# Two layers of a graph network on one core: VectorE's order in the opening, in place of its order at the last two pairs of heads

## The chip, the cores and the metric

The kernel runs on one core of a Trainium2 chip. The metric is the device time in microseconds (us) of one execution. The engines are named as the profile names them: PE is TensorE's matmul, PEld its weight load, DVE VectorE, ACT ScalarE, POOL GpSimd, SP SyncE, which issues the DMAs.

## The reference

The inputs are x of 64 x 256 x 512 (batch, node, feature), a 256 x 256 adjacency matrix of zeros and ones, and the weights of two layers. Everything is float32.

```python
def reference(x, adj, ...):
    # layer 0
    mi = einsum('bkd,od->bko', x, W[:, :512])
    mj = einsum('bkd,od->bko', x, W[:, 512:])
    a = adj.astype(x.dtype);  deg = a.sum(axis=1)
    x = layernorm(x + deg[None, :, None] * (mi + b) + einsum('ij,bjo->bio', a, mj))
    # layer 1: attention with 8 heads of 64, masked by adj
    q, k, v = heads(x @ Wq.T + bq), heads(x @ Wk.T + bk), heads(x @ Wv.T + bv)
    s = where(adj == 0, -inf, (q @ k.T) / 8)
    return layernorm(x + merge(softmax(s) @ v) @ Wo.T + bo)
```

## The kernel before, in words

The 64 batches are taken in 32 groups g of two. `unshifted_path` does all the work; a second path (`general_path`) is entered only for inputs that the first can't take, and does not run here. Matrix products of 2 x 2 blocks are done in Winograd's way, with seven block products in place of eight, so each product needs sums of blocks on both sides: on the left A11, A12, A22 and the sums S1 to S4, on the right B11, B21, B22 and the differences T1 to T4.

**Layer 0 of one batch.** x is split into a rounded part xhi (ACT, L368) and the remainder xlo (POOL, L370), so that the product with the graph is exact; then POOL adds degb, the bias times the degree, to x in place (L373). The graph product of each of four chunks c goes to a PSUM bank (`pa`), 4 instructions a chunk. `take_input` copies three of its blocks to SBUF (xl, ACT, L486) and forms S1, S3, S2 and S4 on DVE (L489 to L492), each from one operand in PSUM; a bank is free when its last sum has read it. Then seven steps (`l0_steps`) multiply these by blocks of the weights w0, 8 matmul instructions each, into banks named x, w, y and z; steps 1 and 3 share x, 4 and 6 share y, 5 and 7 share z, so step 6 writes the bank that step 4's add has read, and step 7 that of step 5's. The results are added into xh on DVE (L530) and, for step 1, through a copy u1 on POOL (L538). Steps 6 and 7 end with the layer norm of a half each.

**The opening** does layer 0 of batch 0 with nothing to hide behind. SP loads, in this order, the graph, x of batch 0, the blocks B11 of the weights, the bias b_bc, T3, B22, B21 (the slot T3 holds a raw block at first), x of batch 1, and later the raw weights of layer 1. DVE forms the differences T1, T2, T4 (L880) ahead of the sums, and T3 (L882) after them. `first_inputs` multiplies all four chunks by xhi first, then by xlo, two chunks in the banks of the scores and two in the pool of three common banks. `check_graph` (L352 to L356) compares the graph with its float32r copy and makes the mask. `make_factors` forms differences of layer 1's weights on DVE (L411) and stores them to DRAM.

**One turn of the loop** over g: it runs attention over the 8 pairs of heads of group g (`scores`, `values`, divisions by the sums), and in between, as pieces of a list `work`, layer 0 of the two batches of group g + 1. At the last two pairs, `divide_at_once` takes two reciprocals (L815) and two products (L816) that complete aoT, the left factor of the output projection; its blocks' sums S1, S2, S3, S4 are formed on DVE (L470 to L473) into oS. The projection's steps (`o_steps`: first A11, A12, A22, then S2, S1, S3, S4) stand among steps 4 to 7 of layer 0 and the transposes of its result; the first is added by POOL through a copy u1 (L698, L699), the others by DVE (L692). `end_values` adds the reciprocals to rtot on POOL (L821). Then follow q, k and v of group g + 1.

**What sets the order.** A planner in the framework orders the instructions of each engine: those whose operands it believes to be ready, earlier in program order first. `in_order` pins an instruction behind the one traced just before it on its engine; `anywhere` leaves it free. All matmuls are pinned. The planner also gives a tile its buffer from those of its pool that are free. In the kernel before, the last two pairs read as below; `left_steps` makes S1, S2, S3, S4, all pinned, and the adds of steps 4 and 5 of layer 0 are pinned too:

```python
left = left_steps(oS[g], in_order)
run(o[:1] + rest[:1] + o[1:2] + left[:1] + rest[1:2] + left[1:])
end_values(inverses)
run(rest[2:] + o[2:5] + work[SLOTS + 1] + o[5:6] + work[SLOTS + 2] + o[6:])
```

where `o` are the projection's steps and `rest` the steps 4 to 7 of layer 0.

Of the kernel before, what the change touches and what calls it, by code (L numbers as in the profile page):

```python
# [16 lines left out]
P = 128  # L17
# [208 lines left out]
def unshifted_path(ctx, tc, flag, x, adj, wiT, wjT, b0, wqT, bq, wkT, bk, wvT, bv, woT, bo, out):  # L226
# [42 lines left out]
    def score_banks(name):  # L269
        return ps_s.tile([P, 2, 512], F32, tag="sc", name=name)  # L270


    def in_order(ins):

        tc.keep_in_program_order(ins)
# [13 lines left out]
    xh = {}  # L289

    def load_x(b):
        if b < B:
            xh[b] = p6.tile([P, NT, D], F32, tag="xh", name="xh")
            nc.sync.dma_start(out=xh[b], in_=x[b].rearrange("(t p) d -> p t d", p=P))
# [4 lines left out]

    for n, w, j in ((B11, wiT, 0), (T3, wiT, 1), (B22, wjT, 1), (B21, wjT, 0)):  # L300
        nc.sync.dma_start(out=w0[:, n], in_=w.rearrange("(c p) o -> p c o", p=P)[:, :, j * H:(j + 1) * H])
        if n == B11:
            nc.sync.dma_start(out=b_bc, in_=b0.to_broadcast([P, D]))
    load_x(1)


    ident = const.tile([P, P], F32, name="ident")
# [21 lines left out]
    def diagonal(t):  # L329
        return slice(2 * t * P, (2 * t + 1) * P)  # L330

    def edges(t):
        return slice((1 - t) * P, (3 - t) * P)
# [3 lines left out]
    for t in range(NT):  # L337
        pt = bank("pt_a")[:, :N]
        for i in range(NT):
            transpose(pt[:, i * P:(i + 1) * P], a[:, i, t * P:(t + 1) * P], ident)  # L340

        nc.vector.tensor_copy(graph[:, t, edges(t)], pt)
        nc.scalar.copy(aT[:, t, :], pt)

    inexact = const.tile([P, 1], F32, name="inexact")

    def check_graph():


        exact = p1.tile([P, NT, 3 * P], F32, tag="oS", name="exact")  # L350
        for t in range(NT):
            nc.vector.tensor_copy(exact[:, t, edges(t)], aT[:, t, :])  # L352
            nc.vector.tensor_scalar(exact[:, t, diagonal(t)], ident, deg[:, t:t + 1], None, ALU.mult)
        nc.vector.tensor_tensor(exact, exact, graph.bitcast(F32), ALU.not_equal)
        nc.vector.tensor_reduce(inexact, exact.rearrange("p t n -> p (t n)"), AX.X, ALU.max)
        nc.vector.tensor_scalar(maskT, aT, 0.0, MASK, ALU.is_equal, ALU.mult)  # L356

    def degree_bias():
        for t in range(NT):
            in_order(nc.vector.tensor_scalar(degb[:, t, :], b_bc, deg[:, t:t + 1], None, ALU.mult))  # L360

    xhi, xlo, xl, xS, hT, hS, qT, kT, vv, aoT, oS = ({} for _ in range(11))

    def split_x(b):

        if b < B:
            xhi[b] = p1.tile([P, NT, D], F32R, tag="xhi", name="xhi")
            in_order(nc.scalar.copy(xhi[b], xh[b]))  # L368
            xlo[b] = p1.tile([P, NT, D], F32R, tag="xlo", name="xlo")
            in_order(nc.gpsimd.tensor_tensor(xlo[b], xh[b], xhi[b].bitcast(F32), ALU.subtract))  # L370
            if b == 0:
                degree_bias()
            in_order(nc.gpsimd.tensor_tensor(xh[b], xh[b], degb, ALU.add))  # L373


    def load_bias(b, name):
# [89 lines left out]
        return {"A11": a11, "A12": a12, "A21": a21, "A22": a22,  # L466
                "S1": s[:, 0], "S2": s[:, 1], "S3": s[:, 2], "S4": s[:, 3]}

    def left_steps(f, order=anywhere):
        return [lambda: order(nc.vector.tensor_add(f["S1"], f["A21"], f["A22"])),  # L470
                lambda: order(nc.vector.tensor_sub(f["S2"], f["S1"], f["A11"])),
                lambda: order(nc.vector.tensor_sub(f["S3"], f["A11"], f["A21"])),
                lambda: order(nc.vector.tensor_sub(f["S4"], f["A12"], f["S2"]))]  # L473


    def input_tiles(b):
# [28 lines left out]
    def first_inputs(b):  # L505

        input_tiles(b)
        pas = [score_banks("pa")[:, 0, :] if c < 2 else bank("pa") for c in range(NC)]
        for k, part in enumerate((xhi[b], xlo[b])):
            for c in range(NC):  # L510
                for t in range(NT):
                    graph_product(b, c, pas[c], k * NT + t, t, part)
                if k == 1:
                    take_input(b, c, pas[c])

    def l0_steps(b):
        banks = {}

        def product(name, lname, n, first):
            if first:  # L520
                banks[name] = bank("po")[:, :H]
            for c in range(NC):
                matmul(banks[name], xS[b][lname][:, c, :], w0[:, n, c, :], start=(first and c == 0),
                                 stop=(c == NC - 1), skip_group_check=True)

        def place(t, j):
            return xh[b][:, t, j * H:(j + 1) * H]

        def add_to(dst, src, order=anywhere):
            order(nc.vector.tensor_add(dst, src, dst))  # L530

        def step1():
            product("x", "A11", B11, True)
            u1 = p2.tile([P, H], F32, tag="lu", name="u1")
            nc.scalar.copy(u1, banks["x"])

            rest = xh[b].rearrange("p t (j o) -> p (t j) o", j=2)[:, 1:]
            nc.gpsimd.tensor_tensor(rest, rest, u1.unsqueeze(1).to_broadcast([P, 3, H]), ALU.add)  # L538

        def step2():  # L540
            product("w", "A22", T4, True)
            add_to(place(1, 0), banks["w"])

        def step3():
            product("x", "A12", B21, False)
            add_to(place(0, 0), banks["x"])

        def step4():
            product("y", "S2", T2, True)
            add_to(place(0, 1), banks["y"], in_order)  # L550

        def step5():
            product("z", "S1", T1, True)
            add_to(place(1, 1), banks["z"], in_order)

        def step6():
            product("y", "S3", T3, False)
            h = xh[b][:, 1, :].rearrange("p (j o) -> p j o", j=2)
            add_to(h, banks["y"].unsqueeze(1).to_broadcast([P, 2, H]))
            norm(xh[b][:, 1, :])  # L560

        def step7():
            product("z", "S4", B22, False)
            add_to(place(0, 1), banks["z"])
            norm(xh[b][:, 0, :])

        return [step1, step2, step3, step4, step5, step6, step7]

    def h_transpose(b, t, borrow=False):

        g, i = divmod(b, NB)
        if i == 0 and t == 1:
            hT[g] = p1.tile([P, NC, NB * N], F32, tag="hT", name="hT")
            hS[g] = pair_blocks(hT[g], "hS")
        pt = (score_banks("pt_h")[:, 0, :] if borrow else bank("pt_h")).rearrange("p (c n) -> p c n", c=NC)
        for c in range(NC):
            transpose(pt[:, c, :], xh[b][:, t, c * P:(c + 1) * P], ident)
        nc.scalar.copy(hT[g][:, :, i * N + t * P:i * N + (t + 1) * P], pt)
        if t == 0 and i == NB - 1:
            for step in left_steps(hS[g]):  # L580
                step()

    def add_output_bias(b):

# [289 lines left out]
    raw_q, raw_k = load_raw(wqT, "kT"), load_raw(wkT, "oS")  # L874
    load_x(2)
    raw_v, raw_o = load_raw(wvT, "v"), load_raw(woT, "aoT")
    split_x(0)
    w0s = [w0[:, n] for n in range(7)]
    for n, m, k in ((T1, T3, B11), (T2, B22, T1), (T4, B21, T2)):
        in_order(nc.vector.tensor_sub(w0s[n], w0s[m], w0s[k]))  # L880
    first_inputs(0)
    in_order(nc.vector.tensor_sub(w0s[T3], w0s[B22], w0s[T3]))  # L882
    p, q = l0_steps(0), l0_steps(1)
    run([p[0], p[2], p[1]])
    split_x(1)
    run(p[3:5])
    bias_steps()
    make_factors(wqT, "wq", raw_q)
    run(p[5:])
# [30 lines left out]
    for g in range(NG - 1):  # L920
        load_x(NB * (g + 2))
        load_x(NB * (g + 2) + 1)
        work = layer0(g + 1)
        run(work[0])
        for w in range(2, NB * NC, 2):
            values(g, w - 2)
            values(g, w - 1)
            multiply()
            divide_two(g, w - 1)
            later = [scores(g, w), scores(g, w + 1)]  # L930
            part = work[w // 2]
            n = 0 if w == NB * NC - 2 else 1
            run(later[:n] + part[:1] + later[n:] + part[1:])
        w = NB * NC - 2
        values(g, w)
        values(g, w + 1)
        multiply()
        inverses = divide_at_once(g, w + 1)
        o = o_steps(g)
        rest = work[SLOTS]  # L940
        left = left_steps(oS[g], in_order)
        run(o[:1] + rest[:1] + o[1:2] + left[:1] + rest[1:2] + left[1:])
        end_values(inverses)
        run(rest[2:] + o[2:5] + work[SLOTS + 1] + o[5:6] + work[SLOTS + 2] + o[6:])
        end = finish_steps(g)
        q = qk_steps(g + 1, qT, "qT", bq_sb, bqd)
        k = with_output_bias(g + 1, qk_steps(g + 1, kT, "kT", bk_sb, bkd))
        v = v_steps(g + 1)
        run(q[:5] + end[:1] + q[5:6] + end[1:2] + q[6:7] + end[2:3] + k[:1] + end[3:4] + k[1:] + end[4:] + v[:1])
        split_x(NB * (g + 2))  # L950
        run(v[1:5])
        run([scores(g + 1, 0), scores(g + 1, 1)])
        run(v[5:])
# [93 lines left out]
```

## Time and profile before

| | us |
|---|---|
| median of 6 runs | 3220.16 |
| lowest and highest | 3217.01, 3222.06 |
| the profiled execution's own time | 3221.36 |
| its span, first to last instruction | 3219.2 |

The mean granted clock of PE in the profiled execution is 0.998. The span has an opening of about 31 us up to layer 0 of the second batch, a stretch to about 90 us in which the first q, k and v are made and the weights' factors stored, 31 turns of 99.28 us each, and the last group, which has no next layer 0. A line of the timeline gives start and duration in us, engine, line, operation, the tiles written and read, shapes, count, and in brackets how long the engine stood idle just before and what ended that. A line of the waits gives who waited for whom, the total in us, how often, and the longest.

### The profile page before, as it was taken

To read this page: it belongs to the slowest core of one execution; us is meant where nothing else is said; L and a number is where in the kernel's file an instruction comes from. 1 tells how busy PE (TensorE), PEld (TensorE's weight loads), DVE (VectorE), ACT (ScalarE), POOL (GpSimd) and SP (SyncE) were. 2 spreads that over 40 slices of the span, in tenths; PEclk is the share of its full clock that TensorE was granted. 3 is DMA by queue.
4 is the path that set the end of the run, shared out by engine and by line. 5 is a ranking of instruction groups with operands and counts; after the bars stand their busy time and mean duration, and the time that the engine had idled before them with its cause. 6 is when DMAs were issued, how large, how long until landed. Compare 5 with 4: busy or idle time off the path is not lost. (4 is left out here: it accounts for less than half of the span.)

```text
span 3219.2 us, 48188 instructions
## 1 busy us (share of the span) xinstructions
PE 3180.9 (99%) x17398; PEld 2620.0 (81%) x17398; DVE 1847.2 (57%) x3847; ACT 1108.6 (34%) x2146; POOL 1504.8 (47%) x1191
## 2 busy tenths in 40 slices
PE   7999999999999999999999999999999999999998
PEld 6888888888888888888888888888888888888885
DVE  6655555555565555655555655556555565555655
ACT  2333333333333433333333333333333333333333
POOL 3454444544445444455444454344544445444453
PEclk9999999999999999999999999999999999999999
DMA  7234332333323433223442234432334323333222
GB/s 245 65 107 125 121 95 75 103 118 123 111 65 95 121 122 119 74 87 112 123 123 86 77 107 122 121 106 67 100 119 124 113 69 91 118 121 119 80 71 93
DMA packets 257167, 340.89 MB, mean 106 GB/s; under 512 B 29856, under 2 KB 154272, under 8 KB 256928
## 3 DMA queue, kind: packets, MB, share of 16 engines
q1 hardware_dynamic: 256928, 337.76, 34.2%
q8 instruction: 143, 2.34, 0.3%
q14 instruction: 96, 0.79, 0.1%
HBM read 274.73 MB, written 37.75 MB: 97 GB/s over the span
## 5 line engine op out<-in xcount | busy, mean ns | idle before, releaser
L454 POOL TENSOR_TENSOR rstd<-ve,mhalf 128x1 f32<-128x1 f32 x256 | 139.5, 549 | 802.5 <-DVE below L452 802.5
L281 PE MATMUL po<-w,xS 128*128 128x256 f32 x2048 | 466.2, 381 | 0.5 <-DVE xh L530 0.5
L281 PE MATMUL st<-hS,factor 128*128 128x256 f32 x2048 | 454.4, 380 | 2.7 <-DVE u L637 2.7
L764 POOL TENSOR_TENSOR pk<-pe 128x512 f32<-128x512 f32 x256 | 321.9, 1273 | 276.9 <-ACT pe L761 276.9
L281 PEld LDWEIGHTS po<-w,xS 128*128 128x128 f32 x2048 | 386.7, 190 | 62.6 <-DVE rden L834 10.3
L281 PEld LDWEIGHTS st<-hS,factor 128*128 128x128 f32 x2048 | 390.2, 191 | 56.5 <-DVE u L637 3.1
L281 PE MATMUL po<-w,xl 128*128 128x256 f32 x1536 | 360.4, 384 | 17.3 <-DVE xS L492 16.4
L761 ACT ACTIVATE pe<-pe 128x1024 f32<-128x1024 f32 x256 | 270.2, 1057 | 248.2 <-DVE pe L757 248.2
L281 PEld LDWEIGHTS po<-w,xl 128*128 128x128 f32 x1536 | 284.2, 190 | 73.9 <-PE po L281 23.1
L281 PE MATMUL st<-hT,factor 128*128 128x256 f32 x1536 | 342.2, 379 | 1.0 <-DVE qT L668 1.0
L757 DVE TENSOR_TENSOR pe<-ps,maskT 128x1024 f32<-128x1024 f32 x256 | 297.1, 1201 | 67.6 <-PE ps L281 67.6
L637 DVE TENSOR_TENSOR u<-st,u 128x512 f32<-128x512 f32 x96 | 66.4, 692 | 468.6 <-PE st L281 461.1
L530 DVE TENSOR_TENSOR xh<-po,xh 128x256 f32<-128x256 f32 (+1 forms) x384 | 172.5, 463 | 279.6 <-POOL xh L538 197.0
L281 PEld LDWEIGHTS st<-hT,factor 128*128 128x128 f32 x1536 | 291.7, 190 | 40.9 <-DVE qT L668 1.4
L281 PE MATMUL ps<-qT,kT 64*128 64x256 f32 x2048 | 256.5, 389 | 0.0
L281 PE MATMUL pav<-pe,v_sb 128*64 128x256 f32 x2048 | 250.1, 386 | 1.9 <-ACT pe L761 1.8
L281 PEld LDWEIGHTS ps<-qT,kT 64*128 64x128 f32 x2048 | 187.0, 186 | 68.2 <-issue 51.3
L281 PE MATMUL st<-factor,hS 128*128 128x256 f32 x1024 | 234.8, 382 | 0.0
L281 PE MATMUL st<-factor,oS 128*128 128x256 f32 x992 | 229.4, 379 | 0.0
L692 DVE TENSOR_TENSOR xh<-st,xh 128x512 f32<-128x512 f32 x186 | 144.9, 779 | 134.9 <-PE st L281 133.8
L834 DVE RECIPROCAL rden<-den 128x256 f32<-128x256 f32 x96 | 168.7, 1757 | 92.0 <-PE den L281 86.3
L281 PEld LDWEIGHTS st<-factor,hS 128*128 128x128 f32 x1024 | 191.9, 190 | 35.4 <-issue 10.6
(112 smaller groups left out, 4920.7 us busy)
## 6 DMA issues: line engine op xcount, KB each, us to landing
xh<-in_x_dram SPq DMA_DIRECT2D x64, 512.0 KB, 4.1
factor<-wq SPq DMA_DIRECT2D x128, 256.0 KB, 2.6
factor<-wk SPq DMA_DIRECT2D x128, 256.0 KB, 2.6
factor<-wv SPq DMA_DIRECT2D x128, 256.0 KB, 4.4
factor<-wo SPq DMA_DIRECT2D x124, 256.0 KB, 2.7
out_dram<-xh SPq DMA_DIRECT2D x62, 512.0 KB, 4.1
factor<-in_wqT_dram SPq DMA_DIRECT2D x96, 256.0 KB, 2.7
factor<-in_wkT_dram SPq DMA_DIRECT2D x96, 256.0 KB, 2.7
```

The lines of the kernel that those rows point to most:

```text
L281: in_order(nc.tensor.matmul(*args, **kw))
L454: nc.gpsimd.tensor_tensor(rstd, ve, mhalf, ALU.pow)
L530: order(nc.vector.tensor_add(dst, src, dst))
L637: nc.vector.tensor_add(new("u2"), bank["y"], k["u1"])
L692: nc.vector.tensor_add(dst, src, dst)
L757: nc.vector.tensor_add(pe.rearrange("p j t q -> p j (t q)"), ps.rearrange("p j t q -> p j (t q)"), maskT.rearrange("p t q -> p (t q)").uns ...
L761: in_order(nc.scalar.activation(flat, flat, AF.Exp, scale=QSCALE, accum_out=etot[:, NB * g + i, pr:pr + 1]))
L764: nc.gpsimd.tensor_tensor(pk, pe[:, :, 0, :], pe[:, :, 1, :], ALU.add)
L834: nc.vector.reciprocal(rden, den)
```

## The change

In the opening: x of batch 0 is rounded right after the loads are issued, and the copies of aT on ACT are pinned behind that. The remainder of batch 0 is made on DVE (`remainder(0, nc.vector)`) instead of POOL. The bias b_bc is loaded behind all four blocks of the weights. `first_inputs` takes its chunks in reverse, puts one of them in the bank of the values and only one in the common pool, and returns a function that forms the sums by name: S3 and S2 of all chunks, then S1, then S4. DVE's order is pinned: remainder, T1, T2, T4, the sums S3 and S2, the degree bias, S1, the difference T3, S4. POOL's add of the degree bias follows the sums S3 and S2. The graph check is pinned where it is written, the second batch's split is written in two pieces.

At the last two pairs of heads: `left_steps` becomes `combine_left`, written after step 5 of layer 0, with only S3 pinned; the adds of steps 4 and 5 are no longer pinned.

```diff
@@ loads, in program order
     for n, w, j in ((B11, wiT, 0), (T3, wiT, 1), (B22, wjT, 1), (B21, wjT, 0)):
         nc.sync.dma_start(out=w0[:, n], ...)
-        if n == B11:
-            nc.sync.dma_start(out=b_bc, in_=b0.to_broadcast([P, D]))
+    nc.sync.dma_start(out=b_bc, in_=b0.to_broadcast([P, D]))
     load_x(1)
+    def round_x(b):
+        xhi[b] = p1.tile([P, NT, D], F32R, tag="xhi", name="xhi")
+        in_order(nc.scalar.copy(xhi[b], xh[b]))
+    round_x(0)
...
-        nc.scalar.copy(aT[:, t, :], pt)
+        in_order(nc.scalar.copy(aT[:, t, :], pt))
...
@@ check_graph: each of its instructions is now in_order(...)
...
+    def remainder(b, engine):
+        xlo[b] = p1.tile([P, NT, D], F32R, tag="xlo", name="xlo")
+        in_order(engine.tensor_tensor(xlo[b], xh[b], xhi[b].bitcast(F32), ALU.subtract))
+    def add_bias(b):
+        in_order(nc.gpsimd.tensor_tensor(xh[b], xh[b], degb, ALU.add))
...
-    def left_steps(f, order=anywhere):
-        return [lambda: order(nc.vector.tensor_add(f["S1"], f["A21"], f["A22"])),
-                lambda: order(nc.vector.tensor_sub(f["S2"], f["S1"], f["A11"])),
-                lambda: order(nc.vector.tensor_sub(f["S3"], f["A11"], f["A21"])),
-                lambda: order(nc.vector.tensor_sub(f["S4"], f["A12"], f["S2"]))]
+    def combine_left(f, order=anywhere):
+        nc.vector.tensor_add(f["S1"], f["A21"], f["A22"])
+        nc.vector.tensor_sub(f["S2"], f["S1"], f["A11"])
+        order(nc.vector.tensor_sub(f["S3"], f["A11"], f["A21"]))
+        nc.vector.tensor_sub(f["S4"], f["A12"], f["S2"])
...
@@ first_inputs
-        pas = [score_banks("pa")[:, 0, :] if c < 2 else bank("pa") for c in range(NC)]
+        pas = [score_banks("pa")[:, 0, :], score_banks("pa")[:, 0, :],
+               ps_v.tile([P, 2, N], F32, tag="av", name="pa").rearrange("p r q -> p (r q)"), bank("pa")]
+        f = xS[b]
         for k, part in enumerate((xhi[b], xlo[b])):
-            for c in range(NC):
+            for c in reversed(range(NC)):
                 for t in range(NT):
                     graph_product(b, c, pas[c], k * NT + t, t, part)
                 if k == 1:
-                    take_input(b, c, pas[c])
+                    in_order(nc.scalar.copy(xl[b][:, c].rearrange("p m n -> p (m n)"), pas[c][:, :3 * P]))
+        def add(name, c, x, y, sign):
+            in_order(nc.vector.tensor_tensor(f[name][:, c], x, y, ALU.add if sign > 0 else ALU.subtract))
+        def sums(name):
+            for c in reversed(range(NC)):
+                _, a12, a22, a21 = (pas[c][:, m * P:(m + 1) * P] for m in range(4))
+                if name == "S2":
+                    add("S3", c, f["A11"][:, c], a21, -1)
+                    add("S2", c, a22, f["S3"][:, c], -1)
+                elif name == "S1":
+                    add("S1", c, a21, f["A22"][:, c], 1)
+                else:
+                    add("S4", c, a12, f["S2"][:, c], -1)
+        return sums
...
@@ l0_steps, steps 4 and 5
-            add_to(place(0, 1), banks["y"], in_order)
+            add_to(place(0, 1), banks["y"])
-            add_to(place(1, 1), banks["z"], in_order)
+            add_to(place(1, 1), banks["z"])
...
@@ the opening
-    split_x(0)
+    remainder(0, nc.vector)
+    sums = first_inputs(0)
     w0s = [w0[:, n] for n in range(7)]
     for n, m, k in ((T1, T3, B11), (T2, B22, T1), (T4, B21, T2)):
         in_order(nc.vector.tensor_sub(w0s[n], w0s[m], w0s[k]))
-    first_inputs(0)
+    sums("S2")
+    degree_bias()
+    add_bias(0)
+    sums("S1")
     in_order(nc.vector.tensor_sub(w0s[T3], w0s[B22], w0s[T3]))
+    sums("S4")
     p, q = l0_steps(0), l0_steps(1)
     run([p[0], p[2], p[1]])
-    split_x(1)
+    round_x(1)
+    remainder(1, nc.gpsimd)
     run(p[3:5])
+    add_bias(1)
     bias_steps()
...
@@ the last two pairs of heads
-        left = left_steps(oS[g], in_order)
-        run(o[:1] + rest[:1] + o[1:2] + left[:1] + rest[1:2] + left[1:])
+        run(o[:1] + rest[:1] + o[1:2] + rest[1:2])
+        combine_left(oS[g], in_order)
         end_values(inverses)
```

The sums of hS, left unpinned in both kernels, are written through the same function.

More of the change, by code (lines that the diff above doesn't have):

```diff
@@ L301, in unshifted_path @@
         nc.sync.dma_start(out=w0[:, n], in_=w.rearrange("(c p) o -> p c o", p=P)[:, :, j * H:(j + 1) * H])
-        if n == B11:
-            nc.sync.dma_start(out=b_bc, in_=b0.to_broadcast([P, D]))
+    nc.sync.dma_start(out=b_bc, in_=b0.to_broadcast([P, D]))
     load_x(1)
+    xhi, xlo, xl, xS, hT, hS, qT, kT, vv, aoT, oS = ({} for _ in range(11))
+    def round_x(b):
+        xhi[b] = p1.tile([P, NT, D], F32R, tag="xhi", name="xhi")
+        in_order(nc.scalar.copy(xhi[b], xh[b]))
+    round_x(0)
     ident = const.tile([P, P], F32, name="ident")
@@ L351, in check_graph @@
         for t in range(NT):
[L352 to L356, printed above, removed]
+            in_order(nc.vector.tensor_copy(exact[:, t, edges(t)], aT[:, t, :]))
+            in_order(nc.vector.tensor_scalar(exact[:, t, diagonal(t)], ident, deg[:, t:t + 1], None, ALU.mult))
+        in_order(nc.vector.tensor_tensor(exact, exact, graph.bitcast(F32), ALU.not_equal))
+        in_order(nc.vector.tensor_reduce(inexact, exact.rearrange("p t n -> p (t n)"), AX.X, ALU.max))
+        in_order(nc.vector.tensor_scalar(maskT, aT, 0.0, MASK, ALU.is_equal, ALU.mult))
     def degree_bias():
@@ L360, in degree_bias @@
             in_order(nc.vector.tensor_scalar(degb[:, t, :], b_bc, deg[:, t:t + 1], None, ALU.mult))
-    xhi, xlo, xl, xS, hT, hS, qT, kT, vv, aoT, oS = ({} for _ in range(11))
+    def remainder(b, engine):
[3 more added lines that the diff above has]
+        in_order(nc.gpsimd.tensor_tensor(xh[b], xh[b], degb, ALU.add))
     def split_x(b):
         if b < B:
[L367 to L373, printed above, removed]
+            round_x(b)
+            remainder(b, nc.gpsimd)
+            add_bias(b)
     def load_bias(b, name):
@@ L527, in place, with add_to @@
             return xh[b][:, t, j * H:(j + 1) * H]
-        def add_to(dst, src, order=anywhere):
-            order(nc.vector.tensor_add(dst, src, dst))
+        def add_to(dst, src):
+            nc.vector.tensor_add(dst, src, dst)
         def step1():
@@ L579, in h_transpose @@
         if t == 0 and i == NB - 1:
-            for step in left_steps(hS[g]):
-                step()
+            combine_left(hS[g])
     def add_output_bias(b):
```

## The prediction

> **What bounds the kernel now.** I read four views in this order: the page's busy times, the list of who waited for whom with TensorE (PE) as the waiter, the timeline of the first 36 us, and the timeline of one turn of the loop around the last two pairs of heads. The first fence is the page's line, the second is from the list of waits (total us, times, longest us).
>
> ```profile
> PE 3180.9 (99%) x17398; PEld 2620.0 (81%) x17398; DVE 1847.2 (57%) x3847; ACT 1108.6 (34%) x2146; POOL 1504.8 (47%) x1191
> ```
>
> ```profile
> PE po L281 <- DVE xS L492: 16.4, 32, 4.9
> ...
> PE st L281 <- DVE u L637: 2.7, 1, 2.7
> ```
>
> PE is busy for 3180.9 of 3219.2 us, so a microsecond of VectorE (DVE) or GpSimd (POOL) work counts only where PE stands still for it. PE waits 32 times for the last sums of layer 0 (L492): 4.9 us once, in the opening, and (16.4 - 4.9) / 31 = 0.37 us in each of the 31 turns of the loop. The reciprocals at L815 recur every 99.28 us with hardly any scatter: a turn is paced by PE. So a turn can gain at most that 0.37 us, which lies at the second half of layer 0's inputs, a place that the change does not touch. The loop has something to lose and almost nothing to win; the opening can win.
>
> The opening, from the timeline (start, us, engine, line):
>
> ```profile
> 7.37 2.37 POOL L370 TENSOR_TENSOR xlo<-xh,xhi 128x1024 fp32r<-128x1024 f32 x1 [5.66 <-ACT xhi L368]
> ...
> 10.56 2.38 POOL L373 TENSOR_TENSOR xh<-xh,degb 128x1024 f32<-128x1024 f32 x1 [0.82 <-DVE degb L360]
> 10.60 3.42 DVE L880 TENSOR_TENSOR w<-w 128x1024 f32<-128x1024 f32 x1 [0.18 <-DMA w<-in_wiT_dram]
> ...
> 14.29 3.96 DVE L880 TENSOR_TENSOR w<-w 128x1024 f32<-128x1024 f32 x2
> ...
> 21.17 3.56 PE L281 MATMUL po<-w,xl 128*128 128x256 f32 x8 [4.86 <-DVE xS L492]
> ...
> 24.53 7.20 PE L281 MATMUL po<-w,xS 128*128 128x256 f32 x32
> ```
>
> The first weight difference takes 3.42 us where the same instruction alone takes about 1.1: it starts while POOL's add (10.56 to 12.94) runs and ends 1.08 us after it. The next two end at 18.25, so the 16 sums start at 18.18, the PSUM bank that PE wants comes free late, and PE stands 4.86 us. After that its 8 matmuls start 0.427 us apart instead of 0.216 (the granted clock is 0.83 in the mean of 20 to 30 us).
>
> The end of a turn, from the same view:
>
> ```profile
> 1036.62 1.89 PE L281 MATMUL st<-factor,aoT 128*128 128x256 f32 x8
> 1036.99 2.35 POOL L699 TENSOR_TENSOR xh<-xh,u 128x1024 f32<-128x1024 f32 x1
> 1037.14 0.42 DVE L816 TENSOR_TENSOR aoT<-pav,rden 128x256 f32<-128x256 f32 x1
> 1037.48 0.41 DVE L530 TENSOR_TENSOR xh<-po,xh 128x256 f32<-128x256 f32 x1
> ...
> 1038.35 5.34 PE L281 MATMUL po<-w,xS 128*128 128x256 f32 x24
> ...
> 1038.62 0.69 DVE L692 TENSOR_TENSOR xh<-st,xh 128x512 f32<-128x512 f32 x1 [0.73 <-PE st L281]
> 1039.23 0.68 DVE L470 TENSOR_TENSOR oS<-aoT 128x512 f32<-128x512 f32 x1
> 1039.30 1.19 POOL L821 TENSOR_TENSOR rtot<-rtot,rden 128x256 f32<-128x256 f32 x1
> 1040.28 0.42 DVE L530 TENSOR_TENSOR xh<-po,xh 128x256 f32<-128x256 f32 x1 [0.37 <-PE po L281]
> 1040.62 0.68 DVE L471 TENSOR_TENSOR oS<-oS,aoT 128x512 f32<-128x512 f32 x1
> ```
>
> The 24 matmuls from 1038.35 are steps 5, 6 and 7 of layer 0, 8 each, 0.216 apart: step 7 begins at 1041.80. It goes on in the bank of step 5, so step 5's add (L530 at 1040.28, ending 1040.70) must have read it: 1.1 us to spare. Likewise step 4's add (ends 1037.89) before step 6 at 1040.08. DVE waits 0.73 us before L692 with S1 (L470) pinned behind it, and S1 starts just as POOL's L699 ends at 1039.34.
>
> **The loop's part.** The change takes the pins off the adds of steps 4 and 5 and off S1, S2 and S4; S3 stays pinned behind S2, and the sums are traced behind step 5. It adds and removes no instruction here. What is not pinned goes where the planner believes its operands to be ready, earlier in the text first. How it places such sums is seen at the same sums of hS (L470, L472, L471, then L692, then L473, from 1052.22): as early as the operands allow, with other work slipped in between. Here S1 needs only the second product of L816. In the planner's order it comes ahead of o's second add (L692) if the planner has L816 done before PE has finished that product: in the trace 1037.56 (1037.9 if step 4's add slips in front) against 1038.5. The planner's reciprocals cannot be much slower than real, nor below some 1 us: it put the second sum of rtot (L821) behind L698 and L699, so its second reciprocal ended after u1 was there, about 2.5 us after the first began. So I take the order step 4, S1, L692, S2, S3, step 5, S4.
>
> Now that order with the chip's durations. S1 reads two SBUF tensors and is issued near 1037.9, while L699 holds until 1039.34. By the row of L880 it ends 0.60 after that, at 1039.94, as it does today; what is new is that L692 now stands behind it: 1040.55, S2 1041.15, S3 1041.75, step 5's add 1042.15. Step 7 would begin at 1041.80, so PE waits 0.4; if POOL's rtot sum (0.73 us alone) slips in between S1 and S2, as it can during L692, which reads PSUM (the sums L489 to L492 do too, and keep their 0.28 beside POOL's L796 at 1018.62), some 0.2 more. Behind that the norm is 0.3 to 0.5 later and has 1.7 us of slack (second ACT apply of the first row ends 1046.74, PE needs it at 1048.49): nothing more. I take 0.5 a turn, 31 x 0.5 = 15.5 us. Bounds: 0 if the planner has L692 first (today's timing, a gain being excluded since PE does not wait there); 1.1 if S4 also goes ahead of step 5 (0.6 more); 1.4 if short planned reciprocals put S1 and S2 ahead of step 4's add too, which then misses step 6 at 1040.08.
>
> [...]
>
> **The opening's part**, piece by piece. x rounded first: 0; ACT's rounding starts at 6.24 today, when x lands (6.19), and the copies of aT that go behind it feed nothing early. Remainder on DVE: 7.34 to about 8.5 (1.1 to 1.2, the L880 rows) instead of POOL's 9.74, but PE takes it at 10.07 after 8 half-speed products: 0 again, yet POOL is now idle when the weight differences run. Bias behind the weights: the landings are 1.5 us apart (7.55, 9.05, 10.51, 12.03, 13.51), so T3, B22 and B21 land at about 9.05, 10.5 and 12.0, the bias at 13.5. The three differences then end near 10.2, 11.7 and 13.2 (today 18.25). Chunks reversed: the copy of chunk 0 is the last of ACT's four (ends 12.70 today), so the first product starts 0.7 late, at 12.7; A12 15.0 to 16.7; A22 with T4 16.7 to 18.5, without today's wait. On DVE: 8 sums of 0.2 to 14.8, degree bias 1.3 to 16, four sums to 16.8; then T3's difference stands behind POOL's add of that bias (2.4, to 18.4) and ends at 19.5; the last four sums 20.3. The bank for step 4 frees with the first of these, 19.9 (its bank is chunk 3's), PE having stood 1.4 us. Four steps of 1.73 end at 26.8; today layer 0's next inputs start at 31.35. That is 4.5 us earlier.
>
> Given back: make_factors' four L411 (0.6 each) now meet POOL's second remainder and add (2.4 each); the add of step 6 stands behind them, near 28.6 where the third bank is wanted near 29.0: 0.5. The graph check, now wholly pinned with its mask (0.41) moved to it, stands before step 4 of the second batch, where PE already waits 0.53 at 45.42: 0.4. Left: about 3.5 us. Bounds: +1 (4.5 lost if POOL and DVE block each other further) to -6.
>
> The idle 1.4 us could also halve the clock. The rows: 0.97 us of idleness (67.18) costs one slow step, 2.72 us (78.80) brings half speed for some 8 matmuls, 1.7 us. I take no slowing, as nearer to the first. [...]
>
> **Sum.** The profiled execution took 3221.36 us (span 3219.2 and 2.2 around it), 1.2 above the median 3220.16. On it: 3221.4 + 15.5 - 3.5 = 3233.4; less 1.2, 3232 for the median.
>
> **Rivals.** What a measurement can tell from no change is about 0.2%, 6.4 us.
> (1) Chance 0.38, the forecast: S1 ahead of L692 only, 0.4 to 0.65 a turn, 3229 to 3237.
> (2) Chance 0.22: S4, or S1 and S2, also ahead of the adds, 1.1 to 1.4 a turn, +31 to +40: 3251 to 3260. For it: planned reciprocals may be short. Against: step 5's product is ready (1040.24) just when S3 would end without POOL.
> (3) Chance 0.25: taking the pins off does not change DVE's order where it matters, L692 still comes first, and only the opening counts: 3216.7, within 0.2%. For it: S1 and L692 become ready within 0.6 us of each other.
> (4) Chance 0.15, the faster side: as (3), and the opening's lead also swallows waits after it, of PE at 36.26 (0.41), 67.18 (0.97) and 78.80 (2.72 with 1.7 of half clock). It decides from 2.9 us on top of the 3.5; all of them would make 3211. Against it: each follows work that moves along.
>
> Chances: faster 0.15, within 0.2% 0.25, slower 0.60. The range leaves out most of (4) and the top of (2): 3213 to 3256; the likeliest case alone is 3229 to 3237.
>
> **What would show it.** Right: L470 starting near 1037.9 of a turn and lasting 2 us, L692 behind it, a new wait "PE po <- DVE xh L530" 31 times, 0.4 to 0.65 each; turns of 99.7 to 99.9 us. In the opening L880 at 1.1 to 1.2 us each, the 4.86 gone, layer 0's second inputs near 27. Wrong: turns still at 99.28, or L470 short while POOL runs.

## The result, and the profile after

| | before | after |
|---|---|---|
| median (us) | 3220.12 (36 runs) | 3227.18 (16 runs) |
| lowest, highest | 3216.66, 3223.74 | 3226.81, 3229.16 |
| span of the profiled execution | 3219.2 | 3226.0 |
| reciprocal that opens the last two pairs, first turn, at | 139.29 | 134.62 |
| median turn of the loop | 99.281 | 99.668 |

The ratio is 1.0024, 95% interval 1.0018 to 1.0031: slower by 7 us, a little over what a measurement can tell from no change. The prediction was 3232 us, slower with chance 0.60. The last two rows of the table part the result for the two profiled executions: the loop begins 4.67 us earlier, loses 11.64 us over the 31 turns that follow (0.387 in the median turn), and the last group's first reciprocal comes 6.97 us late.

The page's line of the engines, after:

```profile
PE 3186.6 (99%) x17398; PEld 2615.4 (81%) x17398; DVE 1891.1 (59%) x3848; ACT 1112.0 (34%) x2146; POOL 1502.1 (47%) x1190
```

DVE is busy 44 us longer for one instruction more. That is the sign of a DVE instruction that stands still while it counts as busy: 44 / 31 = 1.4 us a turn, as long as S1 grew (0.68 to 2.09 below).

The list of waits, with PE as the waiter and then, from the same list, with PE's weight load (total us, times, longest us):

```profile
PE po L281 <- DVE xS L501: 11.2, 31, 0.7
...
PE po L281 <- ACT xl L495: 1.9, 1, 1.9
...
PE po L281 <- DVE xS L528: 1.2, 1, 1.2
...
PE po L281 <- DVE xh L557: 0.9, 1, 0.9
```

```profile
PEld po L281 <- DVE xh L557: 17.5, 32, 1.3
```

The 4.9 us of the opening are gone (1.2 at L528 is what is left of them), the 0.36 a turn at layer 0's inputs stayed (L501, before L492), and a wait for DVE's adds into xh (L557, before L530) is new, 31 times in the loop. It stands under the weight load, since the load for step 7's first matmul is what is held; PE's own list has L557 once, with 0.9 us, and would not have shown it.

The opening's timeline, DVE and PE:

```profile
7.39 1.23 DVE L373 TENSOR_TENSOR xlo<-xh,xhi 128x1024 fp32r<-128x1024 f32 x1 [1.47 <-ACT xhi L310]
...
9.40 1.23 DVE L907 TENSOR_TENSOR w<-w 128x1024 f32<-128x1024 f32 x1 [0.78 <-DMA w<-in_wiT_dram]
...
12.40 1.23 DVE L907 TENSOR_TENSOR w<-w 128x1024 f32<-128x1024 f32 x1 [0.28 <-DMA w<-in_wjT_dram]
...
17.21 2.88 DVE L912 TENSOR_TENSOR w<-w 128x1024 f32<-128x1024 f32 x1
...
20.43 7.14 PE L281 MATMUL po<-w,xS 128*128 128x256 f32 x32 [1.17 <-DVE xS L528]
...
33.97 2.37 PE L281 MATMUL po<-w,xl 128*128 128x256 f32 x9 [1.93 <-ACT xl L495]
```

The weight differences take 1.23 us each where the first took 3.42, and the third ends at 13.6, not 18.25. T3's (L912) stands behind POOL's add (16.65 to 19.00) as foreseen. PE has step 4 at 20.43 instead of 24.53, at full clock (granted 1.00 from 20 to 28 us, where before had 0.67 from 20 to 24 and 0.90 from 24 to 28). The last row is a place where time is given back.

One turn, DVE, POOL and the weight load (the first reciprocal of the turn is at 1031.62):

```profile
1035.43 2.36 POOL L725 TENSOR_TENSOR xh<-xh,u 128x1024 f32<-128x1024 f32 x1
...
1036.25 2.09 DVE L479 TENSOR_TENSOR oS<-aoT 128x512 f32<-128x512 f32 x1
...
1037.74 1.18 POOL L847 TENSOR_TENSOR rtot<-rtot,rden 128x256 f32<-128x256 f32 x1
1038.26 0.68 DVE L718 TENSOR_TENSOR xh<-st,xh 128x512 f32<-128x512 f32 x1
1038.86 0.68 DVE L480 TENSOR_TENSOR oS<-oS,aoT 128x512 f32<-128x512 f32 x1
1039.46 0.68 DVE L481 TENSOR_TENSOR oS<-aoT 128x512 f32<-128x512 f32 x1
1040.06 0.41 DVE L557 TENSOR_TENSOR xh<-po,xh 128x256 f32<-128x256 f32 x1
1040.39 0.68 DVE L482 TENSOR_TENSOR oS<-aoT,oS 128x512 f32<-128x512 f32 x1
1040.53 1.59 PEld L281 LDWEIGHTS po<-w,xS 128*128 128x128 f32 x8 [0.53 <-DVE xh L557]
```

S1 (L479) is issued early, stands until POOL's add (L725) is through at 1037.79 and ends 0.55 later. Behind it come o's second add (L718), S2, S3 and only then the add of step 5 (L557), which ends 8.85 us after the turn's first reciprocal; before, it ended 7.5 after it, and step 7 started 8.62 after it. The weight load stands 0.53 us for it; 0.39 of that is lost to the turn.

### The profile page after: what moved, and what is told of

The parts are those of the page before. It is cut to its first block, busy times and chain, and to the rows that moved or that the text cites. A ratio compares the mean times of both kernels' runs of the same rounds, so it can differ in the third digit from the quotient of the medians.

```text
span 3226.0 us, 48220 instructions
## 1 busy us (share of the span) xinstructions
PE 3186.6 (99%) x17398; PEld 2615.4 (81%) x17398; DVE 1891.1 (59%) x3848; ACT 1112.0 (34%) x2146; POOL 1502.1 (47%) x1190
## 5 line engine op out<-in xcount | busy, mean ns | idle before, releaser
L281 PE MATMUL po<-w,xS 128*128 128x256 f32 x2048 | 474.4, 382 | 5.8 <-DVE xS L528 1.2
L281 PEld LDWEIGHTS po<-w,xS 128*128 128x128 f32 x2048 | 383.8, 190 | 78.8 <-DVE xh L557 17.5
L663 DVE TENSOR_TENSOR u<-st,u 128x512 f32<-128x512 f32 x96 | 66.4, 692 | 468.0 <-PE st L281 461.5
L557 DVE TENSOR_TENSOR xh<-po,xh 128x256 f32<-128x256 f32 (+1 forms) x384 | 170.3, 457 | 267.3 <-POOL xh L565 197.9
L468 ACT ACTIVATE shift<-below,rstd 128x1 f32<-128x1 f32 x256 | 75.4, 295 | 416.9 <-POOL rstd L463 410.1
```

The lines of the kernel that those rows point to most:

```text
L281: in_order(nc.tensor.matmul(*args, **kw))
L468: order(nc.scalar.activation(shift, below, AF.Identity, scale=rstd))
L663: nc.vector.tensor_add(new("u2"), bank["y"], k["u1"])
```

## The experiments

"After" is the changed kernel. The experiments ran in three groups, each beside runs of the kernel before: e1 to e4 (before: median 3219.3 us), e5, e7, e8 and m1 (3220.14), e6, e9, e10 and e11 (3219.39). A ratio is that to the kernel before of the same group.

**The two parts, each alone.** After, with the loop's old code (e1, "the opening alone" below):

```diff
-        run(o[:1] + rest[:1] + o[1:2] + rest[1:2])
-        combine_left(oS[g], in_order)
+        left = left_steps(oS[g], in_order)
+        run(o[:1] + rest[:1] + o[1:2] + left[:1] + rest[1:2] + left[1:])
```

and the adds of steps 4 and 5 pinned again:

> The changed kernel with the old order at the last two pairs of heads: sums S1 to S4 pinned, S1 ahead of step 5's add, the adds of steps 4 and 5 pinned. Theory (the loop costs 0.385 us a turn, the opening gives 4.7 us, and the two add up): turns of 99.28 us, first reciprocal of the last two pairs at 134.6 us, 3220.1 - 4.7 = 3215.4 us, ratio to the kernel before 0.9985. Rival (the opening's lead is an effect of the new loop order, or is lost later): first reciprocal near 139 us or a ratio of 1.000.

And the kernel before, with only the loop's new code (e2):

> The kernel before with only the order at the last two pairs of heads changed (sums of oS unpinned but S3, adds of steps 4 and 5 unpinned); its opening is the old one. Theory: turns of 99.66 to 99.67 us, S1 lasting 2.1 us, 3220.1 + 31 x 0.385 = 3232.0 us, ratio 1.0037. Rival (part of the loss comes from the new opening, by a shifted phase of buffers): turns nearer to 99.28 us, ratio under 1.002.

Measured: the opening alone 3215.79 (ratio 0.9989, 0.9980 to 0.9998), turn 99.279, first reciprocal 133.64 where 134.6 was expected; the loop alone 3229.96 (1.0030, 1.0018 to 1.0042), turn 99.664, S1 at 2.08 us in the median. That is -3.5 and +10.7, together +7.2 where both gave +7.1: the parts add up, and the whole loss is the loop's.

**Is it the place of the sums?** After, with S1 to S4 pinned behind step 5's add, the adds left free (e4):

```diff
-        run(o[:1] + rest[:1] + o[1:2] + rest[1:2])
-        combine_left(oS[g], in_order)
+        run(o[:1] + rest[:1] + o[1:2] + rest[1:2] + left_steps(oS[g], in_order))
```

> The changed kernel with all four sums of oS pinned in a row behind step 5's add, the adds of steps 4 and 5 unpinned. DVE's order: step 4's add, L719, step 5's add, S1, S2, S3, S4. Theory (what costs is only that step 5's add stands behind S1 and S1 behind POOL): PE does not wait at step 7; S4 ends near 10.0 us after the first reciprocal, the add of step 6 is 0.7 us later than in the kernel before, inside its slack of 1.7 us; turns 99.28 us, 3215.4 us, ratio 0.9985. Rival (the sums are needed early, as in the old order with S1 ahead of step 5): a new wait of PE at the projection's S2 product or at the transposes, turns over 99.5 us.

Measured: 3215.81 (0.9990, 0.9981 to 0.9999), turn 99.275. Its timeline:

```profile
1033.45 0.69 DVE L719 TENSOR_TENSOR xh<-st,xh 128x512 f32<-128x512 f32 x1 [1.26 <-PE st L281]
...
1034.75 0.42 DVE L557 TENSOR_TENSOR xh<-po,xh 128x256 f32<-128x256 f32 x1 [0.61 <-PE po L281]
1035.09 0.68 DVE L479 TENSOR_TENSOR oS<-aoT 128x512 f32<-128x512 f32 x1
```

DVE again waits for PE here instead of PE for DVE, and S1 takes 0.68. It is the old turn with the change's opening.

**Or the missing pins on the adds?** After, only these pins put back (e10):

```diff
-            add_to(place(1, 1), banks["z"])
+            add_to(place(1, 1), banks["z"], in_order)
```

and the same for step 4:

> The changed kernel with the pins put back on the adds of steps 4 and 5 alone; the sums of oS stay written behind step 5 and unpinned. Theory (what counts is that the first sum stands ahead of the projection's second add and of step 5's add): DVE's order around the sums is that of the changed kernel, so the turn stays at 99.67 and the time near 3227. Rival (the missing pins on the adds are the cause): turn 99.28, time 3216.

Measured: 3227.59 (1.0023, 1.0014 to 1.0032), turn 99.664. Step 4's add now stands behind the second product, not ahead of it; from S1 on the order is that of after, S1 takes 2.08 us, and step 5's add ends at 8.85 again (first reciprocal of this turn at 1032.81):

```profile
1037.44 2.08 DVE L479 TENSOR_TENSOR oS<-aoT 128x512 f32<-128x512 f32 x1
...
1041.25 0.41 DVE L557 TENSOR_TENSOR xh<-po,xh 128x256 f32<-128x256 f32 x1
```

The pins on the adds are not the cause; the sums' place is.

**Is it POOL that holds S1?** After, o's add on POOL in two halves (e3):

```diff
-            nc.gpsimd.tensor_tensor(o, o, k["u1"].unsqueeze(2).to_broadcast([P, NT, 2, H]), ALU.add)
+            for t in range(NT):
+                nc.gpsimd.tensor_tensor(o[:, t], o[:, t], k["u1"][:, t].unsqueeze(1).to_broadcast([P, 2, H]), ALU.add)
```

> The changed kernel with POOL's add of 1024 elements of the output projection (L725, 2.35 us) split into two of 512 (about 1.27 us each), nothing left out. DVE's order stays S1, L718, S2, S3, step 5's add, S4. Theory (S1 waits for the end of the POOL instruction in flight, and step 5's add is late by that): S1 lasts about 1.0 us in place of 2.08, S2 may wait for the second half and last about 1.2; step 5's add ends at 8.5 us after the first reciprocal in place of 8.85; PE's wait there is gone or under 0.1 us; turns 99.28 to 99.4 us, 3215 to 3219 us. Rival (the order alone costs it, three sums ahead of step 5's add): S1 unchanged or not, the add ends where it did, turns 99.67 us, 3227 us.

Measured: 3225.22 (1.0018, 1.0009 to 1.0027), turn 99.592, a miss. S1 did get through before POOL's second half was done (1035.88 against 1037.02); but the time came back further down:

```profile
1034.07 2.95 POOL L726 TENSOR_TENSOR xh<-xh,u 128x512 f32<-128x512 f32 x2
...
1034.88 1.00 DVE L479 TENSOR_TENSOR oS<-aoT 128x512 f32<-128x512 f32 x1
1035.80 0.68 DVE L718 TENSOR_TENSOR xh<-st,xh 128x512 f32<-128x512 f32 x1
1036.40 1.16 DVE L480 TENSOR_TENSOR oS<-oS,aoT 128x512 f32<-128x512 f32 x1
1036.97 1.18 POOL L848 TENSOR_TENSOR rtot<-rtot,rden 128x256 f32<-128x256 f32 x1
1037.48 1.21 DVE L481 TENSOR_TENSOR oS<-aoT 128x512 f32<-128x512 f32 x1
1038.62 0.41 DVE L557 TENSOR_TENSOR xh<-po,xh 128x256 f32<-128x256 f32 x1
```

S1 meets the first half, S2 the second, S3 the sum into rtot (L848). In each case the DVE sum ends 0.55 us after POOL's instruction (1037.02 and 1037.56 for S2; 1038.15 and 1038.69 for S3), as S1 does in after. That named the next edit (e5): as e3, with the rtot sums moved behind step 7's norm and pinned there.

> The changed kernel with the 1024-element add split in two (as in e3) and the two sums of rtot on POOL moved behind step 7's norm; nothing left out, DVE's order as in the changed kernel. In e3 S1 fell from 2.08 to 1.00 us, but S2 (1.16) and S3 (1.21) then waited for the second half and for rtot's sum. Theory (each DVE sum of two SBUF tensors waits for the POOL instruction in flight, whichever it is): S1 1.0, S2 1.15, S3 0.68, step 5's add ends near 8.25 us after the first reciprocal, before PE needs it at 8.62; turns 99.28 us, 3216 us. Rival (the order S2, S3 ahead of step 5's add costs by itself): turns 99.6 us, 3225 us.

Measured: 3216.27 (0.9988, 0.9979 to 0.9997), turn 99.284. Its timeline:

```profile
1031.87 0.98 DVE L479 TENSOR_TENSOR oS<-aoT 128x512 f32<-128x512 f32 x1
...
1033.38 1.15 DVE L480 TENSOR_TENSOR oS<-oS,aoT 128x512 f32<-128x512 f32 x1
1034.45 0.68 DVE L481 TENSOR_TENSOR oS<-aoT 128x512 f32<-128x512 f32 x1
1035.05 0.41 DVE L557 TENSOR_TENSOR xh<-po,xh 128x256 f32<-128x256 f32 x1
```

Step 5's add ends 8.23 after the first reciprocal (at 1027.23 in this turn), in time for 8.62. DVE's order is exactly that of after; only POOL's work stands elsewhere. So the order alone does not cost the 0.39 us: it is the order together with the time that sums of two SBUF tensors take beside POOL. S1 to S3 took 2.09, 0.68 and 0.68 us in after, 1.00, 1.16 and 1.21 in e3, and take 0.98, 1.15 and 0.68 here.

**What in the opening brings the 3.5 us?** All three are the opening alone with one edit. The bias loaded behind B11 again (e6):

```diff
-    nc.sync.dma_start(out=b_bc, in_=b0.to_broadcast([P, D]))
+        if n == B11:
+            nc.sync.dma_start(out=b_bc, in_=b0.to_broadcast([P, D]))
```

> The new opening with the old loop, and only the bias' load put back behind the block B11, so that the three other blocks land 1.5 us later. Theory (the load's place is worth what PE's wait before step 4 grows by): the three differences still take 1.23 us each, but the third ends 1.5 us later (near 14.2 where the opening alone has 12.8), all sums follow, PE waits about 2.7 us instead of 1.2 before step 4, first reciprocal of the loop 1.5 later than with the opening alone (133.64), so near 135.1, or near 136.5 if that wait halves the clock; time 1.5 to 3 us over the opening alone. Rival: the differences are not what PE waits for, first reciprocal within 0.5 of 133.64.

The same, with the degree bias and POOL's add of it put ahead of the weight differences (e7):

```diff
     remainder(0, nc.vector)
+    degree_bias()
+    add_bias(0)
...
     sums("S2")
-    degree_bias()
-    add_bias(0)
```

> e1 (the new opening, the old loop) with the bias loaded early again, and with the degree bias and POOL's add of it put back between the remainder and the weight differences, so that POOL runs beside them. Theory (most of the opening's gain is that the differences no longer meet POOL): the first difference starts near 10.5 and ends near 13 or later in place of 10.6, the other two follow to about 16.5, the last sums move by some 3 us, PE waits over 3 us before step 2 or step 4, layer 0's second inputs start near 30 in place of 27; first reciprocal near 136.5, 3218 to 3219 us. Rival (the gain is the order of the sums and the one bank of the common pool): first reciprocal under 135, 3216 us.

And the remainder on POOL (`remainder(0, nc.gpsimd)`, e9):

> The new opening with the old loop, and only the remainder of batch 0 put back on POOL (2.4 us instead of 1.23). Theory: it ends near 8.9, PE wants it at 9.2; the first difference on DVE, due at 8.5, waits for it by some 0.5 us and the second, due at 10.0, not at all, so first reciprocal 133.6 within 0.5 and the time that of the opening alone. Rival (the engine of the remainder is a part of the gain, since POOL's other work follows it): POOL's add or DVE's differences are late by 1 us or more and the first reciprocal is at 134.6 or later.

Measured: bias early 3217.38 (0.9992, 0.9983 to 1.0001), first reciprocal 135.51 against 133.64; with the collision 3217.45 (0.9992, 0.9983 to 1.0001), 135.27; remainder on POOL 3215.86 (0.9988, 0.9979 to 0.9997), 133.43. With the bias early, PE's timeline reads:

```profile
21.18 8.77 PE L281 MATMUL po<-w,xS 128*128 128x256 f32 x32 [3.10 <-DVE xS L529]
```

The wait before step 4 is 3.10 (the opening alone: 0.97) and the 32 matmuls take 8.77 instead of 7.14, at half clock for a while (granted 0.66 in the mean of 20 to 25 us); of these 3.8 us only 1.6 to 1.9 reach the loop, since later waits take up the rest. For e6 the two forecast starts of the loop (135.1 and 136.5) lie on either side of what came. So the load's place is worth 1.6 us of the 3.5 by the medians, the remainder's engine nothing. The intervals against the kernel before are wider than such differences (0.0009 is 2.9 us); what supports the 1.6 is the longer wait in the trace and the later first reciprocal. The collision that I saw in the trace of before (3.42 us) shows no cost once the bias is early: there the three differences took 5.34 us together, but the degree bias then no longer stood between the sums, and PE waited 3.00. Neither of the two starts of the loop forecast for e7 (136.5, or under 135) came. The remaining 1.9 us (order of the sums, chunks reversed, graph check, rounding) was not parted.

**Where the opening gives back.** The opening alone, with batch 0's norm on ACT put behind the four copies of the second batch's inputs (`run(late)` after `l0_inputs(1, 1)`, e8):

> e1 with ACT's two norm applications of batch 0 pinned behind the four copies of the second batch's inputs; in the changed kernel the fourth copy stands behind the first norm and PE waits 1.9 us for it at 33.97. Theory (that wait is the order on ACT alone): the copy ends near 31.5, PE's wait there is gone, first reciprocal 1.0 to 1.9 us earlier than in e1 (133.6), 3214 to 3215 us. Rival (the transposes of batch 0, which need the norm, become late in turn): PE waits at the transposes instead and the first reciprocal stays within 0.5 us.

Measured: 3215.97 (0.9986, 0.9977 to 0.9995), no gain; first reciprocal 133.68. The rival's number came, but not at the place that it named. The wait for ACT's copy went, and a wait of the same length came, for the sums that read the same bank:

```profile
33.57 1.97 PE L281 MATMUL po<-w,xl 128*128 128x256 f32 x8 [1.86 <-DVE xS L501]
```

**The wait that both kernels have.** PE waits 0.36 us a turn for the bank of layer 0's inputs. I took DVE's mask add for what delays the sums, and pinned the second of the last scores' two adds behind them (m1: the opening alone, with `second(in_order)` at the last scores):

> e1 with one thing more: at the last scores of a turn the second mask add on DVE is pinned behind the sums of layer 0's second half inputs, which hold the bank that PE waits 0.35 us for in every turn of both kernels. Theory (that wait is DVE's order, the sums standing behind two mask adds of 1.2 us): the wait goes, turns 98.85 to 98.95 us, 3202 to 3205 us, ratio 0.9955. Rival (the exponential of the last pair, 1.7 us later, is late for the values): a new wait of PE at pav or den, turns 99.2 us or more.

Measured: 3232.58 (1.0036, 1.0022 to 1.0050), turn 99.833. Its waits:

```profile
PE po L281 <- ACT xl L495: 15.4, 32, 1.9
PE po L281 <- DVE xS L501: 6.3, 31, 0.2
```

The sums' wait fell to 0.2, but 0.43 a turn appeared for ACT's copy: with the add moved, the planner put an exponential ahead of it. The turn grew by 0.55, more than these two rows make, since here too the weight load was held longer than PE (0.83 in the turn at 1024.62), and the product behind it started 0.7 late. A miss: one pin on DVE moved the order of ACT.

Then the other end of the same wait, the bank's last reader: S4 reads A12 from its copy in SBUF (e11, the opening alone otherwise).

```diff
-        nc.vector.tensor_sub(f["S4"][:, c], a12, f["S2"][:, c])
+        nc.vector.tensor_sub(f["S4"][:, c], f["A12"][:, c], f["S2"][:, c])
```

> The new opening with the old loop, and one operand changed: the last sum of layer 0's inputs (S4 = A12 - S2) reads A12 from its copy in SBUF instead of the PSUM bank, so the bank is free one sum earlier. What it could win is the wait of 0.35 to 0.37 us a turn that PE has for that bank, 11 us in all. Theory: the bank's wait goes, since the sum before it ends 0.4 earlier; but S4 now reads two SBUF tensors, so it waits whenever POOL is in an instruction: the first S4 of the second half meets POOL's sum of exponentials (1.2 us, twice in a row) and takes 1 to 2.5 us instead of 0.28. If the work behind it still comes in time the turn is 98.9 to 99.0 and the time near 3206; if the bank of the second chunk, freed 1 to 2 us later, makes PE wait at the next product, the turn is 99.3 to 100.5. I hold the first as a little likelier. Rival (operands in SBUF cost nothing): S4 stays at 0.28 and the turn is 98.92.

Measured: 3207.96 us (0.9963, 0.9950 to 0.9977), turn 98.966: 11.4 us below before, the best of all, and 7.8 below the opening alone. The timeline:

```profile
1017.40 2.56 POOL L791 TENSOR_TENSOR pk<-pe 128x512 f32<-128x512 f32 x2 [2.06 <-ACT pe L788]
1017.49 1.34 DVE L501 TENSOR_TENSOR xS<-xl,xS 128x128 f32<-128x128 f32 x1
...
1019.38 0.72 DVE L501 TENSOR_TENSOR xS<-xl,xS 128x128 f32<-128x128 f32 x1
```

And the opening alone at the same place, with S4's operand in PSUM:

```profile
1019.71 0.28 DVE L501 TENSOR_TENSOR xS<-pa,xS 128x128 f32<-128x128 f32 x1
```

S4 takes 1.34 and 0.72 us in place of 0.28; yet PE's wait for the bank is gone, since the sum ahead of S4 now frees it; in PE's list of waits there is no row for S4 (L501) any more, and four waits for the sum ahead of it (L500), 1.9 us in all. The same hold that costs 0.39 us a turn in the change costs nothing here, where PE does not wait for what is held.

## Why the prediction was right, and where it was off

**The order and the hold.** The order forecast for the sums and adds (S1, L692, S2, S3, step 5's add, S4, in before's lines) is the one in the trace, and so are S1's 2 us, the end 0.55 to 0.6 behind POOL's add, and the wait at step 7. The sign named for that wait, a row of PE's own, did not come: the 31 waits stand under the weight load. The rival that the pins change nothing fell with the turn of 99.668, the rival of two sums more ahead of the adds with it too (+1.1 to 1.4 a turn forecast). That S1 would stand for POOL's add as the first weight difference did (L880, 3.42 us) was an estimate of mine; measured, S1 took 2.09 us beside POOL's add of 2.36, 1.00 beside a half of it (e3), and 0.68 with no POOL instruction under way (e4).

**The size of the loop's term.** This is the step that was off. 0.5 a turn was taken; the median turn grew by 0.387, and the 31 turns together by 11.64 us in place of 15.5. That is 3.9 us of the 4.8 by which 3232 was too high, and it puts the result just under the range of the likeliest case (0.4 to 0.65 a turn, 3229 to 3237). The 0.5 held some 0.1 for POOL's sum into rtot slipping in between S1 and S2. It did slip in (1037.74 to 1038.92), but L718, which has an operand in PSUM, ran beside it in 0.68, and S2 at 1038.86 took 0.68. That the 0.4 below it came so close is in part luck, since two errors nearly cancel. The forecast had step 5's add end 8.97 us after the first reciprocal (1042.15 less 1033.18) and PE need it at 8.62. The add ended at 8.85, but the weight load wants it sooner: with the add at 8.85 (after) and 8.78 (e3) the turn is 0.39 and 0.31 longer, which puts the limit near 8.46, an estimate from these two kernels. The other 0.9 us were not traced; they are within the opening's scatter, for with the same opening the first reciprocal was at 133.6 in one kernel (e1) and at 135.8 in another (e10).

**The opening.** Net -3.5 forecast and -3.5 measured in e1, -4.67 between the two profiled executions; that the net agrees is partly luck. The pieces up to step 4 came nearly as worked out (differences 1.23 against 1.1 to 1.2; the second inputs at 27.23 against 26.8, so 4.1 us earlier and not 4.5). The two forecast losses came, smaller. The third bank, put at 0.5, shows under the weight load, behind step 6's add, and makes PE 0.24 late:

```profile
29.77 0.19 PEld L281 LDWEIGHTS pa<-graph,xhi 128*128 128x128 f32 x1 [0.41 <-DVE xh L557]
```

The graph check, put at 0.4, cost 0.33 (0.86 at 43.47, before 0.53). Not foreseen was a loss of 1.5 at ACT's fourth copy, behind batch 0's norm (1.93 at 33.97, where before waited 0.41 at 36.26). And some of it returned, as these rows of before and of after show (L637 is L663 in after):

```profile
78.80 5.41 PE L281 MATMUL st<-hS,factor 128*128 128x256 f32 x16 [2.72 <-DVE u L637]
```

```profile
75.81 3.72 PE L281 MATMUL st<-hS,factor 128*128 128x256 f32 x16 [1.69 <-DVE u L663]
```

The wait is 1.0 shorter, and the 16 matmuls behind it take 1.7 us less, since the execution of before lost the clock there (granted 0.65 from 80 to 84 us; 1.00 in after). These pieces add up to 4.75, against the 4.67 by which the loop begins earlier. The last is rival (4)'s mechanism, in part; it shows in the profiled execution of before, less in its median.

**The clock.** No slowing was taken for the forecast wait of 1.4, and there was none after 1.17 (granted 1.00 from 20 to 28 us). This too was not certain: with the same opening the wait ahead of step 4 lay between 0.97 and 2.36 us in the profiled executions, and behind the 2.36 (e3) the 32 matmuls took 8.79 us in place of 7.14 (granted 0.59 from 20 to 24 us).

## What to carry to other kernels

Before an order is loosened, list which of the loosened instructions read two SBUF tensors while GpSimd has a long instruction. Here one such sum taken early took 2.09 us in place of 0.68 beside an add of 2.36; what stood behind it on VectorE came later, and the price, 0.39 us a turn, was its wait less the slack of whoever was queued behind, down to the first one that PE wanted. With an operand left in PSUM, the same overlap was free (L718 took 0.68 us beside POOL's 1.18); so it was where the consumer was not awaited (e11: S4 at 1.34 in place of 0.28, and the turn 0.31 shorter). And look for a new wait under the weight load as well as under the matmul: in after 17.5 us stood there, and 0.9 in PE's own list.

## What the runs showed of the hardware that I had not expected

POOL's instructions, too, took longer beside S1. POOL's rtot sum takes 1.18 us in after, where its fellow takes 0.72, and ends 0.58 after S1 does (in before, too, it takes 1.19 at 1039.30, beside S1). With the add halved (e3), the two halves run from 1034.07 to 1037.02, 2.95 us together where one add of that size (L724) takes 1.26, and VectorE's S1 ends at 1035.88, before the second half does.

Half clock followed some of PE's waits and not others, and no length of wait parts the cases. It followed waits of 2.4 (e3, granted clock 0.98 from 16 to 20 us and 0.59 from 20 to 24), 3.00 (e7, 0.64 from 20 to 24 and 0.93 from 24 to 28) and 3.10 us (e6, 0.63 and 0.94) ahead of step 4, and of 4.48 (e2, 0.75 and 0.82) and 4.86 us (before, 0.67 and 0.90) ahead of the product before it, but not one of 2.2 (e11, 1.00); at 78.80 in before it followed 2.72 (0.92 from 76 to 80, 0.65 from 80 to 84), but at the same place not 2.8 in e10 (1.00), the kernel with the pinned adds. In that kernel it followed a wait of 1.93, at another place (0.84 from 32 to 36, 0.74 from 36 to 40):

```profile
33.25 3.56 PE L281 MATMUL po<-w,xl 128*128 128x256 f32 x10 [1.93 <-ACT xl L495]
```

In after, the same wait of 1.93 was followed by full clock (9 matmuls in 2.37, granted 1.00 from 32 to 40). By the same means over 4 us, the time at half clock was about 3.4 us in each of the seven cases (in before 2 x 4 x (0.33 + 0.10) = 3.4 for the first, and 2 x 4 x (0.08 + 0.35) = 3.4 at 78.80). What parts the waits that it followed from the others was not shown.
